# Where the result's scatters are issued in a two-layer graph network on one core

## The chip, the cores and the metric

The kernel runs on one core of a Trainium2 chip. A core has five engines that run side by side, each through its own list of instructions in order: PE (TensorE, matrix products), DVE (VectorE), ACT (ScalarE), POOL (GpSimd) and SP (SyncE, here only issuing transfers). Data move between memory and the on-chip buffers by DMA transfers, which are issued from SP, ACT or POOL. A transfer whose rows are picked by a list of indices (an indirect one: a gather reads such rows, a scatter writes them) is issued from POOL here.

The metric is the device time of one execution, in microseconds (us). It was 4598.26 us, the median of three runs (4597.88 to 4599.86).

## What is computed

A graph of 6250 nodes with 128 features each and 206,250 edges. A first layer spreads the features five times along the edges, then projects and normalises. A second layer is an attention over the edges of each node. Cut to what matters:

```python
def _L1_gnn_ref(node_attr, edge_attr, edge_sh, ..., edge_index):
    src, dst = (edge_index[0], edge_index[1])
    q = (node_attr @ Wq).reshape(n, H, DQ // H)
    x_src = node_attr[src]
    k = _conv_per_edge(x_src, edge_attr, edge_sh, Wang_k, Wlin_k, W1k, b1k, W2k)
    v = _conv_per_edge(x_src, edge_attr, edge_sh, Wang_v, Wlin_v, W1v, b1v, W2v)
    alpha = jnp.einsum('ehq,qk,ehk->eh', q[dst], Wdot, k)
    ...                      # softmax of alpha over the edges of each dst
    out = jax.ops.segment_sum(attn[..., None] * v, dst, num_segments=n)
    return out.reshape(n, DV) @ Wout

x = _layernorm(x + _L0_gnn_ref(x, edge_index, L0_gnn_weight, L0_gnn_bias), axis=-1)
x = _layernorm(x + _L1_gnn_ref(x, edge_attr_16, edge_attr_16_n2, ..., edge_index), axis=-1)
return x
```

The change lies in the second layer, at the end of it: how the rows of the final `x` get to memory.

## The kernel before

The first half of the run sorts and counts edges and runs the first layer (`count_rows`, `propagate`). While the first layer runs, `order_nodes` ranks the nodes by their number of edges and `lay_edges` lays the edge data out in that order. In `lay_edges`, the text of the program issues for each tile one gather of source indices (L639, into `src_all`) and one or more gathers of edge rows (L643, into `ea_l`, a tile with six buffers), then writes them back transposed (L668).

The second half is `attend`. Nodes stand in the order of their rank, 128 to a tile, 49 tiles (0 to 48). Tile `t` has `WIDTHS[t]` slots: slot `j` holds the `j`-th edge of each of its 128 nodes. The widths fall from 64 to 22 and sum to 1658. Slots are worked on in groups of up to four that don't cross a tile's end: 433 groups. One loop of iterations `i` runs over the groups, and in each iteration stands, in this order:

- `fetch(i + 3)`: on SP the edge data; on POOL one gather per slot (L788), which brings the 128 source nodes' rows from `x1_d` into `xs`. `xs` has six buffers, one group each. A buffer comes free when its group's transposes are done.
- `nets(i)`, `radial(i - 1)`, `turn(i + 1)`, `keys(i - 1)`: the per-edge products on PE, DVE and ACT. `turn` holds the transposes of the gathered rows (L817), which are the last use of an `xs` buffer.
- `step(running)`, two or three times: carries `softmax(t)` of the tile before one `yield` further. So the softmax of a tile is spread over about nine iterations of the next tile's groups.

At its end `softmax(t)` writes the tile's rows to `z[:, t, :]` (L922, DVE) and their statistics. `z` holds all 49 tiles and is used once. After tiles 12, 25, 38, 45, 47 and 48 (`NORMS`, L47) it normalises all tiles since the last time: L933 on DVE, one instruction per tile, and right behind each L933 the scatter of that tile's 128 rows to `out`, by the node numbers in `rows` (L937, POOL). Batches are thus 13, 13, 13, 7, 2 and 1 scatters. Inside a batch there is a `yield` after every fourth tile (`u % 4 == 3`). The scatters are declared free of one another, since every node has one place.

The order of PE, DVE and ACT is that of the text: L53 names them in `MANUAL`, and the loop runs inside `tc.manual_schedule(engines=MANUAL)`. POOL and SP aren't named there; the order of their lists is made by the compiler, which takes account of what depends on what and of which buffers are free.

Of the kernel before, what the change touches and what calls it, by code (L numbers as in the profile page):

```python
# [18 lines left out]
P = 128  # L19
N = 6250  # L20
# [123 lines left out]
def stats(nc, work, z, v):  # L144
    st = work.tile([P, nc.vector.BN_STATS_DIM], F32, name="st")
    nc.vector.bn_stats(st, z)
    nc.vector.bn_aggr(v, st)
# [567 lines left out]
def attend(tc, w1, b1, wang, w2, wlin, wqd, wout, ident, rows, c_iota, src_all, eas_o, x1_d, x1_r, out):  # L715


    nc = tc.nc
    WM = WIDTHS[0]
    with ExitStack() as s:  # L720
        one = s.enter_context(tc.tile_pool(name="at1", bufs=1))
# [30 lines left out]
        nc.vector.tensor_scalar(none, degf, 0.0, None, OP.is_equal)  # L752
        z = one.tile([P, NT, D], F32, name="z")
        v = one.tile([P, NT, 2], F32, name="v2")
        puts = []
        kvs = [one.tile([P, WIDTHS[i], DK + D], F32, name=f"kv{i}") for i in range(2)]

        groups = [(t, j, min(4, w - j)) for t, w in enumerate(WIDTHS) for j in range(0, w, 4)]
# [3 lines left out]
        def ps(name):  # L762
            return pp.tile([P, CH], F32, name=name, tag="ps")
# [6 lines left out]
        def fetch(g):  # L770
            t, j, n = groups[g]
            if j == 0:
                x1s[t] = three.tile([P, D], F32, name="x1s")
                nc.sync.dma_start(x1s[t], x1_r[t * P:(t + 1) * P, :])
            if j % SC == 0:

                c, s, m = pieces(t)[j // SC]
                ea[t, c] = three.tile([P, 4, SC * 32], FR, name="ea")
                for i in range(8):
                    at = (i % 4 // 2) * 32 + i // 4 * 16  # L780
                    nc.sync.dma_start(
                        ea[t, c][16 * i:16 * i + 16, :, :m * 32].bitcast(F32),
                        bass.AP(tensor=eas_o.tensor, offset=eas_o.offset + (at * OFFS[NT] + s) * P,
                                ap=[[OFFS[NT] * P, 16], [m * 32, 4], [1, m * 32]]))
            xs[g] = deep.tile([P, 4, D], F32, name="xs")
            for i in range(n):
                c = OFFS[t] + j + i
                nc.gpsimd.indirect_dma_start(  # L788
                    out=xs[g][:, i, :], out_offset=None, in_=x1_d[:, :],
                    in_offset=bass.IndirectOffsetOnAxis(ap=src_all[:, c:c + 1], axis=0))  # L790
# [52 lines left out]
        def radial(g):  # L843

            t, j, n = groups[g]
            r = r1.pop(g)
            p_r = pp.tile([P, 2, CH], F32, name="p_r")
            for i in range(n):
                u = i % 2 * (DK + D)
                nc.tensor.matmul(p_r[:, i // 2, u:u + DK + D], r[:, i, :], w2_s, start=True, stop=True)  # L850
            rr[g] = two.tile([P, 4, DK + D], F32, name="rr")
            r2 = rr[g].rearrange("p (b i) f -> p b (i f)", i=2)
            for b, f in banks(n):
                nc.scalar.copy(r2[:, b, :f], p_r[:, b, :f])  # L854

        def keys(g):
# [12 lines left out]
            for b, f in banks(n):  # L869
# [5 lines left out]
            nc.vector.tensor_reduce(al[t][:, j:j + n], a[:, :, :DK].rearrange("p j (h k) -> p j h k", h=H),  # L875
                                    AX.X, OP.add)

        def softmax(t):

            w = WIDTHS[t]  # L880
            a = kv[t]
            l = al.pop(t)[:, :w]
            ex = two.tile([P, WM, H], F32, name="ex")
            m = two.tile([P, H], F32, name="m")
            d = two.tile([P, H], F32, name="d")
            nc.vector.tensor_tensor(l, l, keep[t][:, :w, None].to_broadcast([P, w, H]), OP.min)
            nc.vector.tensor_reduce(m, l.rearrange("p j h -> p h j"), AX.X, OP.max)
            nc.vector.tensor_tensor(l, l, m[:, None, :].to_broadcast([P, w, H]), OP.subtract)
            yield
            nc.scalar.activation(ex[:, :w], l, AF.Exp)  # L890
            yield
            nc.vector.tensor_tensor(ex[:, :w], ex[:, :w],
                                    ok[t][:, :w, None].to_broadcast([P, w, H]), OP.mult)
            nc.vector.tensor_reduce(d, ex[:, :w].rearrange("p j h -> p h j"), AX.X, OP.add)
            nc.vector.tensor_scalar(d, d, none[:, t:t + 1], None, OP.add)
            nc.vector.reciprocal(d, d)
            yield

            for u in range(0, w, 8):
                k = min(8, w - u)  # L900
                av = a[:, u:u + k, DK:].rearrange("p j (h f) -> p j h f", h=H)
                nc.vector.tensor_tensor(av, av, ex[:, u:u + k, :, None].to_broadcast([P, k, H, D // H]),  # L902
                                        OP.mult)
                yield
                if u > 0:
                    nc.vector.tensor_add(a[:, :k, DK:], a[:, :k, DK:], a[:, u:u + k, DK:])
                    yield
            for h in (4, 2, 1):
                nc.vector.tensor_add(a[:, :h, DK:], a[:, :h, DK:], a[:, h:2 * h, DK:])  # L909
            yield  # L910
            av = a[:, :1, DK:].rearrange("p j (h f) -> p j h f", h=H)
            o = two.tile([P, H, D // H], F32, name="o")
            nc.vector.tensor_tensor(o, av[:, 0], d[:, :, None].to_broadcast([P, H, D // H]), OP.mult)
            yield
            tr = ps("tr4")
            nc.tensor.transpose(tr[:, :P], o.rearrange("p h d -> p (h d)"), ident)
            oT = two.tile([P, P], F32, name="oT")
            nc.scalar.copy(oT, tr[:, :P])
            yield
            y = ps("y4")  # L920
            nc.tensor.matmul(y[:, :D], oT, wo, start=True, stop=True)
            nc.vector.tensor_add(z[:, t, :], x1s.pop(t), y[:, :D])  # L922
            stats(nc, two, z[:, t, :], v[:, t, :])
            if t + 1 in NORMS:
                yield
                t0 = NORMS[NORMS.index(t + 1) - 1]
                rs = two.tile([P, NT], F32, name="rs")
                n = t + 1 - t0
                nc.vector.tensor_scalar(rs[:, :n], v[:, t0:t + 1, 1], EPS, None, OP.add)
                nc.scalar.activation(rs[:, :n], rs[:, :n], AF.Sqrt)  # L930
                nc.vector.reciprocal(rs[:, :n], rs[:, :n])
                for u in range(t0, t + 1):
                    nc.vector.tensor_scalar(z[:, u, :], z[:, u, :], v[:, u, 0:1],  # L933
                                            rs[:, u - t0:u - t0 + 1], OP.subtract, OP.mult)

                    k = min(P, N - u * P)
                    st = nc.gpsimd.indirect_dma_start(  # L937
                        out=out[:, :], in_=z[:k, u, :], in_offset=None,
                        out_offset=bass.IndirectOffsetOnAxis(ap=rows[:k, u, 0:1], axis=0)).ins
                    for q in puts:  # L940
                        tc.declare_no_dep(st, q, reason="a node has one place in the order")
                    puts.append(st)
                    if u % 4 == 3:
                        yield

# [2 lines left out]
        def step(of):  # L948
            if of and next(of[0], None) is None and of[0].gi_frame is None:
                of.pop(0)  # L950

        with tc.manual_schedule(engines=MANUAL):
            for i in range(-3, len(groups) + 1):
                live = [0 <= i + x < len(groups) for x in range(-1, 4)]
                if live[4]:
                    fetch(i + 3)
                if live[1]:
                    nets(i)
                step(running)
                if live[0]:  # L960
                    radial(i - 1)
                if live[2]:
                    turn(i + 1)
                step(running)
                if live[0]:
                    keys(i - 1)
                    t, j, n = groups[i - 1]
                    if j + n == WIDTHS[t]:
                        running.append(softmax(t))
                if len(running) > 1:  # L970
                    step(running)
                if live[3] and groups[i + 2][1] == 0:
                    begun.append(begin(groups[i + 2][0]))
                step(begun)
            for r in running:
                for _ in r:
                    pass


def attend_any(tc, w1, b1, wang, w2, wlin, wqd, wout, c_heads, c_sum, ident, last, srct, dstt, eat,  # L980
# [368 lines left out]
```

## Time and profile before

| | us |
|---|---|
| median of three runs | 4598.26 |
| the profiled execution, in all | 4606.73 |
| its span, first to last instruction | 4604.9 |
| attention stage: first gather L788 starts | 2315.69 |
| last gather L788 starts / ends | 4557.74 / 4558.69 |
| last scatter L937 starts | 4592.12 |
| batches of scatters start | 3116.60, 3729.38, 4268.58, 4534.52, 4578.19, 4592.12 |

The busy time of the engines by stage, in us:

| stage (us from the span's start) | PE | DVE | ACT | POOL | granted PE clock |
|---|---|---|---|---|---|
| 0 to 430 (sorting, counting) | 187 | 346 | 111 | 92 | 0.88 |
| 430 to 1005 (edge counts) | 403 | 494 | 334 | 56 | 0.78 |
| 1005 to 2315 (first layer) | 1243 | 948 | 701 | 478 | 0.98 |
| 2315 to 4605 (attention) | 1951 | 1963 | 906 | 1728 | 0.95 |

A row of the list of groups reads: line, engine, operation, what it writes and reads, how many; after the bar the busy time and the mean duration of one in ns; after the next bar the engine's idle time just before these instructions, and what ended it. "issue" is time in which the engine waited for nothing that the profile shows. A row of a timeline reads: start, duration, engine, line, operation, and in brackets the gap before it and what ended the gap. In a row for a stretch the columns after its length are busy time and number of instructions, the granted PE clock, the busy share of the transfer engines and GB/s.

### The profile page before, as it was taken

To read this page: it belongs to the slowest core of one execution; us is meant where nothing else is said; L and a number is where in the kernel's file an instruction comes from. 1 tells how busy PE (TensorE), PEld (TensorE's weight loads), DVE (VectorE), ACT (ScalarE), POOL (GpSimd) and SP (SyncE) were. 2 spreads that over 40 slices of the span, in tenths; PEclk is the share of its full clock that TensorE was granted. 3 is DMA by queue.
4 is the path that set the end of the run, shared out by engine and by line. 5 is a ranking of instruction groups with operands and counts; after the bars stand their busy time and mean duration, and the time that the engine had idled before them with its cause. 6 is when DMAs were issued, how large, how long until landed. Compare 5 with 4: busy or idle time off the path is not lost.

```text
span 4604.9 us, 73118 instructions
## 1 busy us (share of the span) xinstructions
PE 3785.5 (82%) x24823; PEld 3371.9 (73%) x24823; DVE 3751.0 (81%) x5996; ACT 2051.8 (45%) x4137; POOL 2353.1 (51%) x2343
## 2 busy tenths in 40 slices
PE   4345554997999999999868898987888878888886
PEld 4345554886888888787667788887888868787785
DVE  8769996865787787766649898987988988899887
ACT  0046664644656566464334343443443433444333
POOL 0340000056333344303277777777777777777774
PEclk9986766998999999999989999999999999999898
DMA  8023334555877788765365455554555555555442
GB/s 296 9 50 78 80 78 115 150 155 164 238 229 229 222 233 247 230 174 155 111 125 101 98 102 101 103 99 97 102 100 100 106 97 105 102 103 102 90 100 48
DMA packets 389736, 601.64 MB, mean 131 GB/s; under 512 B 120093, under 2 KB 325205, under 8 KB 378554
## 3 DMA queue, kind: packets, MB, share of 16 engines
q1 hardware_dynamic: 256570, 356.98, 32.0%
q0 software_dynamic: 127056, 204.67, 19.4%
q10 hardware_dynamic: 5728, 35.22, 2.3%
q8 instruction: 201, 3.29, 0.3%
q14 instruction: 181, 1.48, 0.1%
HBM read 491.89 MB, written 132.25 MB: 136 GB/s over the span
## 4 chain that ended last, share of the span: by engine, by line
PE 23%; DVE 11%; DMA 8%; POOL 7%; issue 5%; ACT 1%; SPq 0%; DVEq 0%; POOLq 0%; ACTq 0%
DMA xs<-x_d,src_all 7%; PE p_r L850 6%; POOL xs L788 6%; PE p_k L866 5%; PE p_k L864 3%; DVE mkv L839 3%; DVE kv L871 3%; PE acc L444 3%; PE p_g L831 2%; PE p_x L817 1%; DVE kv L902 1%; DVE kv L909 1%; DVE kv L873 1%; PE p_h L831 1%; POOL x_r L368 1%
## 5 line engine op out<-in xcount | busy, mean ns | idle before, releaser
L788 POOL DMA_INDIRECT xs<-x_d,src_all x1658 | 1676.7, 1011 | 505.5 <-issue 423.1
L444 PE MATMUL acc<-c,parts 128*128 128x512 f32 (+1 forms) x6370 | 1411.1, 382 | 78.9 <-DVE c L427 42.8
L444 PEld LDWEIGHTS acc<-c,parts 128*128 128x128 f32 x6370 | 1154.3, 189 | 305.8 <-DVE c L427 48.9
L427 DVE CAST c<-c 128x1024 fp32r<-128x1024 uint8 x980 | 683.8, 716 | 240.1 <-PE acc L444 196.2
L866 PE MATMUL p_k<-wlin_s,mkv 128*128 128x128 f32 x3316 | 755.4, 310 | 0.0
L440 ACT CAST c<-c 128x512 fp32r<-128x512 uint8 x735 | 456.2, 623 | 561.5 <-PE acc L444 441.9
L864 PE MATMUL p_k<-wlin_s,mkv 128*128 128x64 f32 x3316 | 581.1, 258 | 65.7 <-DVE kv L871 64.8
L850 PE MATMUL p_r<-w_s,r 128*128 128x192 f32 x3316 | 619.9, 330 | 0.0
L850 PEld LDWEIGHTS p_r<-w_s,r 128*128 128x128 f32 x3316 | 571.2, 194 | 34.4 <-issue 0.2
L864 PEld LDWEIGHTS p_k<-wlin_s,mkv 128*128 128x128 f32 x3316 | 523.1, 199 | 95.0 <-DVE kv L871 94.1
L871 DVE TENSOR_TENSOR kv<-rr,p_k 128x768 f32<-128x768 f32 (+2 forms) x443 | 397.1, 898 | 205.6 <-PE p_k L866 189.0
L854 ACT COPY rr<-p_r 128x768 f32<-128x768 f32 (+2 forms) x443 | 335.3, 759 | 476.8 <-PE p_r L850 462.2
L839 DVE TENSOR_TENSOR mkv<-p_g,xT 128x512 f32<-128x512 f32 (+3 forms) x866 | 534.2, 659 | 7.0 <-PE p_g L831 6.9
L866 PEld LDWEIGHTS p_k<-wlin_s,mkv 128*128 128x128 f32 x3316 | 523.5, 199 | 0.0
L228 PE MATMUL p_c<-oh_h,oh_l 128*128 128x100 bf16 x3136 | 301.1, 273 | 263.3 <-DVE oh_h L153 199.5
L833 ACT ACTIVATE r<-p_h,b_s 128x512 f32<-128x512 f32 (+3 forms) x433 | 290.6, 671 | 464.1 <-PE p_h L831 456.4
L228 PEld LDWEIGHTS <-oh_l 128*128 128x128 bf16 x3136 | 289.3, 124 | 272.2 <-DVE oh_h L153 208.0
L668 POOL DMA_DIRECT2D eas_o<-eT_l x252 | 204.9, 816 | 505.2 <-DVE eT_l L662 490.7
L817 PE MATMUL p_x<-ident,xs 128*128 128x128 f32 x1658 | 276.9, 279 | 131.7 <-DMA xs<-x_d,src_all 123.2
L230 ACT CAST cT<-p_c 128x500 uint8<-128x500 f32 (+1 forms) x637 | 306.8, 644 | 118.1 <-DVE c_row L236 61.1
L817 PEld LDWEIGHTS p_x<-ident,xs 128*128 128x128 f32 x1658 | 212.2, 142 | 164.4 <-DMA xs<-x_d,src_all 122.6
L820 ACT COPY xT<-p_x 128x512 f32<-128x512 f32 (+3 forms) x433 | 248.6, 574 | 135.9 <-PE p_x L817 131.9
(195 smaller groups left out, 4524.8 us busy)
## 6 DMA issues: line engine op xcount, KB each, us to landing
c<-counts SPq DMA_DIRECT2D x360, 384.0 KB
ea<-eas_o SPq DMA_DIRECT2D x648, 128.0 KB
c<-counts SPq DMA_DIRECT2D x120, 448.0 KB
eas_o<-eT_l POOLq DMA_DIRECT2D x162, 256.0 KB
counts<-c_row SPq DMA_DIRECT2D x588, 48.0 KB
xs<-x_d,src_all POOLq DMA_INDIRECT x1658
eat<-in_eas ACTq DMA_DIRECT2D x1, 25792.0 KB
counts<-c_row SPq DMA_DIRECT2D x196, 56.0 KB
```

Source lines behind the costliest of these rows:

```text
L228: nc.tensor.matmul(p_c[:, q - q0], oh_los[t % 2][:, q // Q, :, q % Q], oh_hi[:, q // Q, :, q % Q], start=True, stop=True)
L427: nc.vector.tensor_copy(c[:, u:u + 1024].rearrange("p (n b x) -> p n b x", n=2, b=2), r[:, :, v:v + 512].rearrange("p b (n x) -> p n b x", ...
L440: nc.scalar.copy(c[:, 1024:w].rearrange("p (b x) -> p b x", b=2), r[:, :, 512:])
L444: nc.tensor.matmul(a[:, :v - u], parts[:, j, i, :], c[:, u:v], start=(j == 0 and i == 0), stop=(j == NT - 1 and i == 1))
L788: nc.gpsimd.indirect_dma_start(out=xs[g][:, i, :], out_offset=None, in_=x1_d[:, :], in_offset=bass.IndirectOffsetOnAxis(ap=src_all[:, c:c ...
L817: nc.tensor.transpose(p_x[:, i * P:(i + 1) * P], xs[g][:, i, :], ident)
L839: nc.vector.tensor_tensor(mkv[g][:, i, :n].rearrange("p j (b e) -> p b j e", b=4), p_g[:, i, :n * P].rearrange("p (b j e) -> p b j e", b=4 ...
L850: nc.tensor.matmul(p_r[:, i // 2, u:u + DK + D], r[:, i, :], w2_s, start=True, stop=True)
L854: nc.scalar.copy(r2[:, b, :f], p_r[:, b, :f])
L864: nc.tensor.matmul(p_k[:, i // 2, u:u + DK], m[:, 0, i, :], wlin_s[:, :DK], start=True, stop=True)
L866: nc.tensor.matmul(p_k[:, i // 2, u + DK:u + DK + D], m[:, 1, i, :], wlin_s[:, DK:], start=True, stop=True)
L871: nc.vector.tensor_mul(k.rearrange("p (b i) f -> p b (i f)", b=b.stop - b.start), r2[:, b, :f], p_k[:, b, :f])
```

## The change

`softmax` no longer issues a tile's scatter behind its L933. It notes the tile in a list `done`. A new function `store` issues the scatters of the noted tiles and empties the list. The loop calls it at the end of an iteration only from `i + 3 >= len(groups)` on, that is once no `fetch` follows in the text, and then behind each further step of the softmaxes that are still running. The instruction itself is the same, and so are its operands and the declaration that scatters are free of one another.

```diff
-        puts = []
+        puts, done = [], []
...
+        def store():
+
+            for u in done:
+
+                k = min(P, N - u * P)
+                st = nc.gpsimd.indirect_dma_start(
+                    out=out[:, :], in_=z[:k, u, :], in_offset=None,
+                    out_offset=bass.IndirectOffsetOnAxis(ap=rows[:k, u, 0:1], axis=0)).ins
+                for q in puts:
+                    tc.declare_no_dep(st, q, reason="a node has one place in the order")
+                puts.append(st)
+            done.clear()
...
                 for u in range(t0, t + 1):
                     nc.vector.tensor_scalar(z[:, u, :], z[:, u, :], v[:, u, 0:1],
                                             rs[:, u - t0:u - t0 + 1], OP.subtract, OP.mult)
-
-                    k = min(P, N - u * P)
-                    st = nc.gpsimd.indirect_dma_start(
-                        out=out[:, :], in_=z[:k, u, :], in_offset=None,
-                        out_offset=bass.IndirectOffsetOnAxis(ap=rows[:k, u, 0:1], axis=0)).ins
-                    for q in puts:
-                        tc.declare_no_dep(st, q, reason="a node has one place in the order")
-                    puts.append(st)
+                    done.append(u)
                     if u % 4 == 3:
                         yield
...
                 step(begun)
+                if i + 3 >= len(groups):
+                    store()
             for r in running:
                 for _ in r:
-                    pass
+                    store()
+                store()
```

## The prediction

> **What bounds the kernel now.** I read the list of groups for POOL alone over the attention stage first, then the table of waits of that stage, then POOL's timeline at the places where the scatters stand.
>
> ```profile
> 2315.60:4558.70 2243.10, 1723.77 (x1704) 0.96 0.53 101
> L788 POOL DMA_INDIRECT xs<-x_d,src_all x1658 | 1676.7, 1011 | 505.5 <-issue 423.1 <-DMA xs<-x_d,src_all 38.9 <-PE p_x L817 21.9
> L937 POOL DMA_INDIRECT out<-z,rows x49 | 50.7, 1035 | 45.3 <-DVE z L933 31.0 <-issue 7.0 <-DMA out<-z,rows 2.7
> POOL xs L788 <- issue: 423.1, 1388, 0.4
> ```
>
> The first line is POOL's busy time from the first gather to the end of the last: 1723.77 us in 1704 instructions (1658 gathers and 46 scatters) of 2243.10. The remaining 519.3 us are 1704 gaps of 0.305 us. The last line gives the longest such gap as 0.4 us: POOL never stands still for a buffer, an engine or a transfer. A gather costs 2181.0/1657 = 1.316 us from start to start, and POOL's chain of 1704 issues sets when the last gather leaves. Other engines have room: in the same stretch PE is busy 1937 us and DVE 1935 us of 2243 (86%), and PE's transposes at L817 wait 123.2 us for gathered rows in the run. After the last gather 46.2 us remain.
>
> ```profile
> 3095.69 2.15 DVE L933 TENSOR_SCALAR z<-z,v,rs 128x128 f32<-128x128 f32 x8
> ...
> 3115.08 1.21 POOL L788 DMA_INDIRECT xs<-x_d,src_all  x1 [0.30 <-issue]
> 3116.60 1.01 POOL L937 DMA_INDIRECT out<-z,rows  x1 [0.31 <-issue]
> ...
> 3125.84 1.20 POOL L937 DMA_INDIRECT out<-z,rows  x1 [0.30 <-DMA out<-z,rows]
> 3127.34 0.99 POOL L788 DMA_INDIRECT xs<-x_d,src_all  x1 [0.30 <-PE p_r L850]
> 3128.64 0.99 POOL L788 DMA_INDIRECT xs<-x_d,src_all  x1 [0.30 <-issue]
> 3129.94 1.00 POOL L937 DMA_INDIRECT out<-z,rows  x1 [0.30 <-issue]
> ```
>
> Start, duration, engine, line; the bracket is the gap before. Eight scatters, two gathers, five scatters. Counting POOL's rows from 2315.69, 611 gathers lie before the first scatter. The program text has it elsewhere: tile 12's normalisation falls in iteration 151, by which `fetch` has issued groups 0 to 154, that is the 583 slots of tiles 0 to 13 and 12 more, 595. The 16 extra gathers are groups 155 to 158. Group 158 takes the buffer of group 152, whose transposes (`turn(i+1)`) stand in iteration 151: POOL's list had run as far ahead as the six `xs` buffers allow. The next two batches stand after 1063 and 1461 gathers, in the text after 1047 and 1445: again 16 more. The fourth begins after 1646 (text 1632), in the middle of the last group the buffers allow.
>
> So the compiler orders POOL (it isn't among the `MANUAL` engines of L53) by what is ready, not by place in the text. A second place shows how far it goes:
>
> ```profile
> 1035.37 1.02 POOL L643 DMA_INDIRECT ea_l<-eat,at_l  x1 [0.30 <-issue]
> 1036.70 1.02 POOL L639 DMA_INDIRECT src_all<-srct,at_l  x1 [0.30 <-issue]
> 1038.02 1.19 POOL L639 DMA_INDIRECT src_all<-srct,at_l  x1 [0.30 <-issue]
> ...
> L639 POOL DMA_INDIRECT src_all<-srct,at_l x49: 950/955/1829, 1025.2 to 1102.9; - x49
> L643 POOL DMA_INDIRECT ea_l<-eat,at_l x126: 957/1080/1705, 1027.4 to 1946.0; - x126
> ```
>
> In the text each L639 stands just ahead of its tile's first L643. In the trace six L643 go out (their tile has six buffers), then L639 of later tiles run one after another: all 49 by 1102.9, while the L643 go on to 1946.0. When the loop has no free buffer, work that needs none is drawn forward from far behind it.
>
> **The change part by part.** The 49 scatters are the same instructions with the same operands. In the text 46 of them move behind all 1658 gathers; the last three (tiles 46 to 48) already stand there. Nothing is added on PE, DVE, ACT or SP: their lists hold the same instructions in the same order.
>
> (a) *The move.* A scatter needs its row block of `z` (L933) and nothing that is scarce: no `xs` buffer. The eight L933 from 3095.69 run in 2.15 us without waiting for any scatter between them in the text, although they write the same tile: the dependence goes by region. So scatter 0 is ready in the compiler's order where it was, and POOL's list was out of gathers there. I expect the first 39 in the same stretches, at most spread over several groups because a freed buffer's gathers now go first. They stay ahead of the last gather: 0 us.
>
> (b) *The last batch.* Tiles 39 to 45 have ten gathers left behind them:
>
> ```profile
> 4534.52 1.00 POOL L937 DMA_INDIRECT out<-z,rows  x1 [0.30 <-issue]
> 4535.82 0.98 POOL L788 DMA_INDIRECT xs<-x_d,src_all  x1 [0.30 <-issue]
> ...
> 4544.78 0.97 POOL L937 DMA_INDIRECT out<-z,rows  x1 [0.30 <-issue]
> 4546.05 0.99 POOL L788 DMA_INDIRECT xs<-x_d,src_all  x1 [0.30 <-PE p_k L866]
> ...
> 4557.74 0.95 POOL L788 DMA_INDIRECT xs<-x_d,src_all  x1 [0.30 <-issue]
> 4578.19 1.10 POOL L937 DMA_INDIRECT out<-z,rows  x1 [19.50 <-DVE z L933]
> 4579.60 1.00 POOL L937 DMA_INDIRECT out<-z,rows  x1 [0.31 <-DVE al L888]
> 4592.12 1.57 POOL L937 DMA_INDIRECT out<-z,rows  x1 [11.53 <-DVE z L933]
> ```
>
> Each of the seven that slips behind the last gather lets that gather out one scatter earlier. The 46 scatters take 61.0 us start to start, 1.327 each. From none to all seven: 0 to -9.3 us. Behind the last gather they cost nothing as long as the 19.50 us gap (waiting for DVE's z of tile 46) covers them, and 9.3 fits; without that gap they would cost the 9.3 back. Six of them stood in one stretch between groups 429 and 430, so the nearest row says that nearly all stay; I take one: -1.3.
>
> (c) *Changes of kind on POOL.* The first instructions after a change between gathers and scatters are longer: 1.01 and 1.02 against 0.97 for scatters (the first batch), 0.99 and 0.99 against 0.95 for gathers, together 0.17 us a visit. There are six visits now before the last gather, at most 46 if every scatter stood alone: 0 to 40 x 0.17 = +6.8. Six and thirteen scatters stood together before without a gather between them, so I take 0.
>
> (d) *Waits.* POOL runs in order, so a scatter that waits holds up the gathers queued behind it, and PE's L817 behind those. Now scatter 0 starts 20 us after its z began (3095.69 to 3116.60) and is not waited for. At unchanged places that stays: 0. If the compiler put them about 16 gathers sooner, the margin would be gone; but they can't be ready sooner than now.
>
> Sum: 4604.9 + 0 - 1.3 + 0 + 0 = 4603.6 us of span. The profiled execution took 4606.73 in all, 8.5 above the median of 4598.26; taking the difference over to the median, 4598.26 - 1.3 = 4597.0.
>
> One rule of the Trainium skill bears on what a moved issue is worth. DMA: Bandwidth & Descriptors, section "Anatomy of one DMA", puts most of a small DMA's fixed 2 us in the completion, with about 50 ns for the sequencer and little for building descriptors; as an estimate from that, 46 issues would hold POOL for 46 x 0.05 = 2.3 us and no order of them could matter. The rows here say 0.97 us busy and 0.30 between, 61.0 us for the 46; the measurement decides.
>
> **The rivals.**
>
> *The order follows the text (faster).* Then the last gather leaves 61.0 us sooner, 46 scatters follow it back to back from 4558.99 - 61.0 = 4498.0 to 4559.0, then tiles 46, 47 and 48, whose z is ready by 4592.1 - 61.0 = 4531.1, at 1.33 each. The last would start at 4561.7, where it now starts at 4592.12; with the same 12.8 us after it the span is 4574.4, -30.5: 4567.8 of median. For it: the text, and a POOL that never idles. Against it: the two places above where POOL's order departs from the text as soon as buffers run out.
>
> *The order follows the text and the gathers were not what held the stage (slower).* Then PE or DVE takes over as bound, and the last gather doesn't leave sooner; it waits for a buffer instead. All 49 scatters would follow it, the last at 4558.99 + 48 x 1.327 = 4622.7 in place of 4592.12: +30.6, 4628.9. It turns from gain to loss where the last gather gains less than 30.6 of the 61.0 us. For it: PE and DVE at 86%, and a granted clock that falls at times. Against it: 61 us is 2.7% of the stage, less than the 14% that they have free, and the transposes wait on gathers now.
>
> **How the numbers follow.** My forecast, that the compiler draws the scatters forward and little changes, has a chance of 0.84; the text's order with its gain 0.10; with its loss 0.06. The time is the forecast's, 4597. Its ends are -9.3 and +6.8 on 4598.26, 4589.0 and 4605.1; with 1 us for the spread of the three runs, 4588 to 4606. That leaves out the two rivals, 0.16, and little more, so it is the range. About 0.2% (9.2 us) is what a measurement of this kernel can tell from no change. Faster by more: 0.10 from the rival and 0.01 from the forecast's lower end; slower by more: 0.06; the same: 0.83.
>
> **What would show it.** In the changed kernel's POOL timeline: the first scatter after about 611 gathers, near 3116, and batches near 3729 and 4268; the last gather near 4557; after it at most seven scatters and then a gap of 10 to 19 us before tile 46's. If a run of 46 scatters follows the last gather, step (a) is wrong, and the time then tells which rival. If scatters stand alone between groups and the rows near them are longer, (c) was undersized. If POOL shows a gap of several us before a scatter with DVE z as the releaser, (d) was.

## The result and the profile after

Over 12 executions of each kernel, side by side, the kernel before took 4599.12 us and the changed one 4601.09 (medians): ratio 1.0003, 95% interval 0.9994 to 1.0013. That is no change that can be measured. The forecast was 4597.0, in a range of 4588 to 4606.

The profiled execution of the changed kernel has a span of 4603.1 us (4604.9 before). The scatter has become L883, its L933 has become L946. First the row of the stage, from the first gather to the end of the last; its columns are length, then busy time and instructions of PE, its weight loads, DVE, ACT and POOL, then the clock, the share of the transfer engines and GB/s:

```profile
2315.20:4556.80 2241.60, 1943.54 (x13114) 1780.47 (x13115) 1935.37 (x3429) 896.44 (x1509) 1722.17 (x1704) 0.96 0.52 101
```

The groups of POOL in the same stretch, and its waits there (total, how many, longest):

```profile
L788 POOL DMA_INDIRECT xs<-x_d,src_all x1658 | 1675.1, 1010 | 505.7 <-issue 426.1 <-DMA xs<-x_d,src_all 37.2 <-PE p_x L817 19.5
L883 POOL DMA_INDIRECT out<-z,rows x46 | 47.1, 1024 | 14.0 <-issue 6.1 <-DMA xs<-x_d,src_all 1.8 <-DVE kv L871 1.5
```

```profile
POOL xs L788 <- issue: 426.1, 1397, 0.3
```

1704 instructions lie in the stretch, as before: 1658 gathers and still 46 scatters. No scatter has left the stage. POOL is still without a pause (519.4 us of gaps, 0.305 each, the longest 0.3), and the stretch is 1.5 us shorter than before (2241.60 against 2243.10).

POOL's timeline shows where the scatters went. The first batch, and the end of the run:

```profile
3113.30 1.22 POOL L788 DMA_INDIRECT xs<-x_d,src_all  x1 [0.30 <-issue]
3114.82 1.00 POOL L883 DMA_INDIRECT out<-z,rows  x1 [0.30 <-issue]
...
3124.06 1.20 POOL L883 DMA_INDIRECT out<-z,rows  x1 [0.30 <-DMA out<-z,rows]
3125.57 0.98 POOL L788 DMA_INDIRECT xs<-x_d,src_all  x1 [0.31 <-PE p_r L850]
...
3129.41 0.95 POOL L788 DMA_INDIRECT xs<-x_d,src_all  x1 [0.30 <-issue]
3130.67 1.00 POOL L883 DMA_INDIRECT out<-z,rows  x1 [0.30 <-issue]
3131.98 0.99 POOL L883 DMA_INDIRECT out<-z,rows  x1 [0.30 <-DMA xs<-x_d,src_all]
...
4548.12 1.00 POOL L883 DMA_INDIRECT out<-z,rows  x1 [0.30 <-issue]
4549.43 1.09 POOL L788 DMA_INDIRECT xs<-x_d,src_all  x1 [0.30 <-DMA xs<-x_d,src_all]
...
4555.85 0.95 POOL L788 DMA_INDIRECT xs<-x_d,src_all  x1 [0.31 <-issue]
4576.32 1.09 POOL L883 DMA_INDIRECT out<-z,rows  x1 [19.52 <-DVE z L946]
4577.71 0.98 POOL L883 DMA_INDIRECT out<-z,rows  x1 [0.30 <-DVE al L901]
4590.23 1.57 POOL L883 DMA_INDIRECT out<-z,rows  x1 [11.54 <-DVE z L946]
```

Counted through, the scatters stand behind these numbers of gathers:

| | first batch | second | third | fourth | last three |
|---|---|---|---|---|---|
| before | 611: 8, 613: 5 | 1063: 13 | 1461: 13 | 1646: 1, 1648: 6 | 1658 |
| after | 611: 8, 615: 2, 619: 3 | 1063: 4, 1067: 6, 1071: 3 | 1461: 7, 1465: 6 | 1648: 6, 1652: 1 | 1658 |

The change of the text has split the batches into portions between groups of four gathers, and nothing else. Ten portions stand ahead of the last gather, where six stood before; behind it are the same three scatters.

### The profile page after: what moved, and what is told of

It reads as the page before. It is cut to its first block, busy times and chain, and to the rows that moved or that the text cites. A ratio compares the mean times of both kernels' runs of the same rounds, so it can differ in the third digit from the quotient of the medians.

```text
span 4603.1 us, 73118 instructions
## 1 busy us (share of the span) xinstructions
PE 3795.4 (82%) x24823; PEld 3382.2 (73%) x24823; DVE 3749.5 (81%) x5996; ACT 2047.5 (44%) x4137; POOL 2352.0 (51%) x2343
## 4 chain that ended last, share of the span: by engine, by line
PE 21%; DMA 9%; DVE 9%; POOL 8%; issue 6%; ACT 1%; POOLq 0%; DVEq 0%; ACTq 0%
DMA xs<-x_d,src_all 9%; POOL xs L788 7%; PE p_r L850 5%; PE p_k L866 5%; PE p_k L864 3%; PE acc L444 3%; DVE mkv L839 2%; DVE kv L871 2%; PE p_g L831 2%; PE p_x L817 1%; PE p_h L831 1%; DVE kv L922 1%; DVE kv L915 1%; DVE kv L873 1%; POOL x_r L368 1%
## 5 line engine op out<-in xcount | busy, mean ns | idle before, releaser
L864 PE MATMUL p_k<-wlin_s,mkv 128*128 128x64 f32 x3316 | 580.9, 258 | 56.6 <-DVE kv L871 55.4
L850 PE MATMUL p_r<-w_s,r 128*128 128x192 f32 x3316 | 623.1, 331 | 0.0
L850 PEld LDWEIGHTS p_r<-w_s,r 128*128 128x128 f32 x3316 | 575.2, 195 | 35.4 <-issue 0.4
L871 DVE TENSOR_TENSOR kv<-rr,p_k 128x768 f32<-128x768 f32 (+2 forms) x443 | 396.7, 897 | 205.5 <-PE p_k L866 189.3
```

What stands on the lines that cost most here:

```text
L864: nc.tensor.matmul(p_k[:, i // 2, u:u + DK], m[:, 0, i, :], wlin_s[:, :DK], start=True, stop=True)
L871: nc.vector.tensor_mul(k.rearrange("p (b i) f -> p b (i f)", b=b.stop - b.start), r2[:, b, :f], p_k[:, b, :f])
```

## The experiments

The mechanism to be tested has two halves. One: the compiler puts a scatter where POOL has run out of gathers that have a free buffer, whatever the text says. The other is the price: what it would have been worth if the scatters had really gone behind the gathers (the faster rival's -30.5 us). Twelve runs were made in four groups, each group on one chip together with the kernel before. On these chips the kernel before took 5091.44, 5098.53, 5136.94 and 5095.58 us, not 4599. So each kernel is compared with the kernel before of its own group, and what differs there is taken up first.

**The kernel before, on such a chip.**

> The kernel before, for its profile on this chip. If this chip hands work over between engines later than the one of the first profile, the gathers' stage takes some 2600 us from first to last gather (2242 in the first profile) with POOL waiting some 200 us for PE's transposes; if POOL is without gaps also here, the 490 us more lie in the stages ahead of 2315.

One execution, 5143.69 us. The stage's row and POOL's waits in it:

```profile
2369.00:5069.90 2700.90, 2095.84 (x12980) 1902.66 (x12981) 1923.96 (x3385) 874.21 (x1492) 1723.54 (x1704) 0.89 0.42 84
```

```profile
POOL xs L788 <- issue: 431.7, 1391, 4.5
POOL xs L788 <- PE p_x L817: 279.0, 111, 6.7
POOL xs L788 <- remote: 131.2, 64, 6.0
```

What lies ahead of the first gather is 53 us longer (2369.00 against 2315.69), the gathers' stage 458 us (2700.90 against 2243.10), what follows the last gather 26 us (72.0 against 46.2). POOL's busy time is the same (1723.54 against 1723.77), and DVE's within 1%; POOL now waits 279.0 us for the transposes that free `xs`, and 131.2 us for something that the profile shows only as "remote". POOL is no longer without gaps here. The counts of gathers ahead of the scatters are those of the first profile. The whole kernel after had the same counts too, and no other time than before:

> The kernel after, unchanged, beside the kernel before on this chip. The theory that the compiler keeps the place of the scatters: 0.999 to 1.001 of the kernel before, portions at 611, 1063, 1461 and 1648 gathers. If the places mattered only where the queue of the gathers has gaps: up to 0.5% off.

Measured: 5134.95 us, ratio 0.9994 (0.9973 to 1.0015), portions behind 611, 615, 619, 1063, 1067, 1071, 1461, 1465, 1648 and 1652 gathers. So the case's result holds on this chip also.

**Does the number of buffers set the place?** The changed kernel with two more `xs` buffers:

```diff
-        deep = s.enter_context(tc.tile_pool(name="at_x", bufs=6))
+        deep = s.enter_context(tc.tile_pool(name="at_x", bufs=8))
```

> The changed kernel with eight xs buffers in place of six. Theory (the compiler draws scatters forward where its gathers run out of buffers): the first scatters stand after 611 + 8 = 619 gathers, the next after 1071 and 1469, in similar portions; the time is as before within 0.2%, since POOL issues as many instructions ahead of the last gather. Rival (their place is set by when z is ready and has nothing to do with the buffers): first scatters still after about 611.

Measured: 5092.47 us, ratio 1.0009 (0.9989 to 1.0028). The batches begin behind 619, 1071, 1469 and 1656 gathers: each exactly eight later, two groups of four. If the readiness of `z` alone set the place, it would have stayed at 611. In the order that the compiler makes, a scatter comes up once the gathers with a free buffer are used up. One of the fourth batch's seven now stands behind the last gather.

**The scatters really behind the gathers.** Each scatter is bound behind the last gather in POOL's list:

```diff
+                gathers.append(nc.gpsimd.indirect_dma_start(
...
-                st = nc.gpsimd.indirect_dma_start(
+                with (tc.issue_after(gathers[-1]) if u >= 0 else ExitStack()):
+                    st = nc.gpsimd.indirect_dma_start(
```

> The changed kernel, with each scatter bound in POOL's issue order behind the last gather, so that the order which the change's text has is also the order that POOL gets. Theory (POOL's chain of issues sets the attention stage, and the change did nothing because the compiler drew the scatters forward): 1658 gathers stand in one run, then 49 scatters; the last gather leaves 61 us sooner, near 4497, the 31 us that POOL idles behind it (19.5 and 11.5) are filled with scatters, span about 4574, 30 us or 0.66% faster than before. Rival (the gathers are not what held the stage; PE or DVE bound): the last gather stays near 4557, the scatters come behind it, up to 31 us slower. Second rival (scatters cost POOL nothing that matters): no change.

> The same kernel as e1_all_behind once more. There the kernel before took 5091 us in place of 4599, POOL waited 244 us for PE's transposes to give buffers free, and engines waited up to 27 us for one another while scatters went out. If this run shows POOL without gaps in the attention stage again (the kernel before near 4599), the theory of the POOL chain asks for -30 us, 0.66% faster. If hand-offs between engines are held up by a burst of scatters also there, the burst of 46 behind the last gather holds up the last groups and the gain is lost: 0 to 30 us slower than that. If the kernel before is near 5090 again, no change, as in e1_all_behind.

> The kernel after with all 49 scatters bound behind the last gather, a third time, for a chip where the kernel before takes 4600 us as in the first profile, if the run falls on such a one. There POOL issues without a gap, and a portion of scatters holds no hand-over between the other engines up: the faster rival's sum says 4568, ratio 0.993. If the tail gives back there too what the stage gains, the ratio is 1.000 as in the two runs before, and this is expected (0.997 to 1.001) on a chip where the kernel before takes over 5050 us.

Measured, on three chips: ratios 0.9992 (0.9972 to 1.0012), 0.9987 (0.9971 to 1.0003) and 0.998 (0.9958 to 1.0002). In each trace all 49 scatters stand behind 1658 gathers. The move that the text describes is done; each interval holds 1 and shuts out the 30 us (ratio 0.994). Where the gain went is seen beside the next kernel, which leaves the rows of tiles 0 to 45 unwritten:

```diff
             for u in done:
+                if u < 46:
+                    continue
```

> The changed kernel without the scatters of tiles 0 to 45; those rows of the result are not written. It measures what 46 scatters cost where they stand. Theory: 46 issues of 1.33 us leave POOL's chain, the last gather goes out 61 us sooner and the 46 us behind it stay as they are: span about 4542, 1.3% faster than before. Rival (stage not bound by POOL): less than half of that.

> The same kernel as e3_left_out once more (without the scatters of tiles 0 to 45). With POOL's chain as the bound: 61 us less, 1.3%. With POOL waiting for buffers and the kernel before near 5090: 1.1% less, as in e3_left_out.

Measured: ratios 0.9888 (0.9863 to 0.9914) and 0.988 (0.986 to 0.990), or 58 and 65 us less for 46 scatters. The last gather of POOL's timeline, first with the scatters behind, then without them on the same chip:

```profile
4955.92 0.95 POOL L788 DMA_INDIRECT xs<-x_d,src_all  x1 [0.30 <-issue]
```

```profile
4964.29 1.02 POOL L788 DMA_INDIRECT xs<-x_d,src_all  x1 [0.30 <-issue]
```

So the stage of the gathers gains about all that taking the scatters out of it can give (the 8 us between the two are less than executions of one kernel differ by there, 5072.67 to 5122.95 for the kernel before). But the span goes on for 129.0 us after the last gather with them behind it, and 64.6 us without them. The second chip shows the same: last gathers at 4971.59 and 4959.68, and 122.0 and 68.5 us behind them. The row of the stretch with the 46 scatters, and that of the rest (all behind, first of its three runs):

```profile
4957.20:5016.30 59.10, 14.77 (x62) 12.78 (x63) 9.01 (x17) 4.04 (x7) 45.37 (x46) 0.61 0.16 51
5016.30:5085.90 69.60, 27.48 (x163) 23.84 (x161) 41.26 (x83) 15.58 (x26) 3.61 (x3) 0.67 0.02 5
```

For 59.1 us POOL issues scatters, and DVE does 17 instructions; the 69.60 us that follow are a whole tail again (64.60 us without the scatters). Rows picked from the timeline of the same stretch show the other engines' waits:

```profile
4958.06 0.69 ACT L833 ACTIVATE r<-p_h,b_s 128x512 f32<-128x512 f32 x1 [0.51 <-PE p_x L817]
...
4959.60 0.44 PE L866 MATMUL p_k<-wlin_s,mkv 128*128 128x128 f32 x2
...
4963.72 0.80 ACT L854 COPY rr<-p_r 128x768 f32<-128x768 f32 x1 [4.98 <-remote]
...
4967.75 2.76 PE L850 MATMUL p_r<-w_s,r 128*128 128x192 f32 x8
...
4980.03 0.95 DVE L871 TENSOR_TENSOR kv<-rr,p_k 128x768 f32<-128x768 f32 x1 [16.86 <-remote]
...
5013.56 0.80 ACT L854 COPY rr<-p_r 128x768 f32<-128x768 f32 x1 [26.55 <-remote]
...
5015.30 0.97 POOL L884 DMA_INDIRECT out<-z,rows  x1 [0.30 <-issue]
5059.36 1.07 POOL L884 DMA_INDIRECT out<-z,rows  x1 [43.09 <-DVE z L947]
```

DVE's L871 at 4980.03 needs `rr` (written by 4964.52) and `p_k` (done by 4960.04): it starts 15.5 us after both. ACT's copy at 5013.56 takes a `p_r` that ended at 4970.51, and L871 had read both `rr` buffers by 4980.98; ACT had stood idle for 26.55 us. The instructions of DVE and ACT last as long as elsewhere (0.95, 0.80). PE's eight L850 take 2.76 us in place of 1.46 at 4954.34, at a granted clock of 0.61 in this stretch; these 1.3 us don't make up the 15 to 26. What is late is the hand-over between engines, as long as POOL issues without a pause. The Trainium skill, SBUF — State Buffer, section "SBUF: two separate sides", names one way in which POOL can block others: it and DVE share a pair of ports, which POOL's and some of DVE's instructions lock for their whole length, while PE and ACT have their own. That doesn't fit here: ACT is held too, by 26.55 us, DVE's own instructions aren't longer, and no scatter of the stretch lasts more than 1.69 us.

**Part of them behind.** Only the scatters of tiles 35 to 48 are bound behind the last gather (`if u >= 35`), eleven more than the three that always stood there:

> The changed kernel, with only the scatters of tiles 35 to 45 (eleven) bound behind the last gather; the others stay where the compiler puts them. Theory (what is won is POOL idle time behind the last gather that gets filled): eleven issues of 1.33 us, 14.6 us, fit into the 19.5 us of idle, so the last gather leaves 14.6 us sooner and the end with it: 0.32% faster than before. Rival (it is the batches of 13 in the middle of the stage that hurt, by starving PE): no gain here, or only a part of it.

> The same kernel as e5_eleven_behind once more (eleven scatters bound behind the last gather). With POOL's chain as the bound: 14.6 us less, 0.32%. With POOL waiting for buffers and the kernel before near 5090: no change.

Measured: 0.9997 (0.998 to 1.0015) and 0.9982 (0.9966 to 0.9998). The 14.6 us of the theory would be a ratio of 0.9971; the first interval shuts that out, the second doesn't. On the chip of the two traces above the last gather starts at 5006.45, 50.5 us later than with all behind, and what remains after it is 76.4 us against 129.0. The 35 scatters that stay ahead cost the stage about what they save the tail.

**One at a time.** If it were long portions that hold the others up, single scatters should be cheaper. The first 39 are each bound to a gather of their own:

```diff
+                at = (620 + 34 * u if u < 13 else 1070 + 30 * (u - 13) if u < 26 else 1465 + 14 * (u - 26))
+                with (tc.issue_after(gathers[at]) if u < 39 else ExitStack()):
```

> The kernel after, but each of the first 39 scatters is bound to a gather of its own: about one scatter after every 34, 30 and 14 gathers of the three stretches, instead of portions of 6 to 8; the last ten as they are. If a scatter costs its own time of the queue wherever it stands (46 left out brought 57 to 65 us), the median is that of the kernel before within 0.3%. If it is the portions that hold up the other engines (in the run of 49 behind the gathers the others waited 26 and 47 us for events that were past), singles cost less: 0.4 to 0.8% below the kernel before.

Measured: 0.9995 (0.9978 to 1.0011), with 39 scatters alone between gathers in the trace. So on these chips a scatter costs about its own time of POOL's queue, alone or in a portion, ahead of the last gather or behind it: 58 and 65 us for 46 of them are 1.3 to 1.4 us each, the time from one to the next.

**The order of the text.** Both rivals supposed that POOL follows the text. The kernel before, with all of POOL's gathers and scatters bound to each other in the order of its text:

```diff
+                with (tc.issue_after(issued[-1]) if issued else ExitStack()):
+                    ld = nc.gpsimd.indirect_dma_start(
...
+                issued.append(ld)
...
+                    with tc.issue_after(issued[-1]):
+                        st = nc.gpsimd.indirect_dma_start(
...
+                    issued.append(st)
```

> The kernel before with POOL's gathers and scatters bound in the order of its text (8 scatters after 595 gathers, 5 more by 599, 13 by 1051, 13 by 1445, 10 by 1630, 3 at the end). The theory that a scatter costs its own time wherever it stands: the kernel before within 0.3%. If the order of the text is what hurts (a scatter ahead of its z holds the gathers behind it): 1 to 3% slower, with POOL's idle time ahead of the scatters put down to DVE's z.

Measured: 5193.51 us, ratio 1.0104 (1.0085 to 1.0124), 56.6 us more than the kernel before. The first scatter of each batch in POOL's timeline:

```profile
3327.35 1.08 POOL L940 DMA_INDIRECT out<-z,rows  x1 [16.93 <-issue]
...
4082.13 1.11 POOL L940 DMA_INDIRECT out<-z,rows  x1 [15.90 <-DVE z L935]
...
4745.63 0.99 POOL L940 DMA_INDIRECT out<-z,rows  x1 [20.43 <-DVE z L935]
...
5080.35 1.00 POOL L940 DMA_INDIRECT out<-z,rows  x1 [17.14 <-DVE z L935]
```

POOL stands four times, 70.4 us together, for a `z` that isn't there yet, with the gathers queued behind the scatter. The first is put down to "issue", but L935 writes its `z` from 3326.19 on, 1.2 us before it starts. In the kernel before the same scatters start without a wait. Bound like this, the batches begin behind 595, 1047, 1441 and 1628 gathers; in the kernel before behind 611, 1063, 1461 and 1646. The 16 to 20 gathers by which the compiler runs ahead (16 x 1.3 = 21 us) are what covers this wait. The 56.6 us aren't that wait alone: behind the first batch DVE and ACT stand 18.56 and 24.63 us for something "remote" while POOL issues gathers, so the price may be another on a chip like that of the first profile.

## Why the prediction held

**Step (a), the move: shown.** The batches stand behind 611, 1063, 1461 and 1648 gathers, starting at 3114.82, 3729.66, 4270.17 and 4535.35, where the prediction named 611 and times near 3116, 3729 and 4268. The spread over several groups is there too. The run with eight buffers shows its reason, that the place is set by free buffers. One count of the prediction is off: in the text the third and fourth batch begin behind 1441 and 1628 gathers, as the run in the order of the text shows, not 1445 and 1632; only the rest of each batch stands there. So the compiler is 16 to 20 gathers ahead, not 16 throughout. Nothing in the sum rests on it.

**Step (b), the last batch: -1.3 taken, 0 found.** None of the seven slipped behind the last gather; the end of its range with no slip was right. The last gather starts at 4555.85 in place of 4557.74; these 1.9 us are less than executions of one kernel differ by (before: 4594.97 to 4609.86). For the same reason the 1 us that the range allowed for spread was too little for single executions (after: 4595.26 to 4612.38); the median lies inside.

**Step (c), changes of kind: right within what shows.** There are ten visits before the last gather in place of six, four more; at 0.17 each 0.7 us. The gathers went out every 1.315 us from start to start, 1.316 before.

**Step (d), waits: 0, shown, and its warning too.** No scatter waits longer than 0.31 us until the gathers are out. The prediction held that the margin of some 20 us would be gone if the scatters stood 16 gathers sooner; the text's order does just that and waits 15.9 to 20.4 us at each of four places.

**The rivals.** Neither happened, as the order doesn't follow the text. Their prices were tried where the order was forced. The faster rival's -30.5 didn't come: the stage of the gathers gave about what it said (50.5 us between 35 scatters ahead and none), but the sum had the last tiles' `z` ready 61 us sooner while the scatters run, and on those chips little runs beside them. The slower rival's reason, gathers that gain less than half, didn't come either. The three ratios have a mean of 0.9986, about 7 us; each interval holds 1.

**What stays open.** Whether -30.5 us could be had on a chip like that of the first profile. There, the other engines go on while a portion is issued, and stand behind it. The second batch of 13 scatters in the kernel before and the 17.2 us that follow, with the same columns, of the first profile and then of the profile on an experiments' chip:

```profile
3729.40:3746.60 17.20, 9.09 (x62) 7.90 (x60) 14.63 (x26) 4.92 (x8) 13.24 (x14) 0.95 0.17 51
3746.60:3763.80 17.20, 11.29 (x58) 9.85 (x59) 3.51 (x7) 3.05 (x6) 13.24 (x14) 0.65 0.20 53
```

```profile
4079.20:4096.40 17.20, 11.57 (x57) 10.28 (x55) 8.70 (x21) 3.78 (x5) 13.20 (x14) 0.71 0.17 51
4096.40:4113.60 17.20, 10.09 (x51) 9.61 (x52) 7.14 (x11) 4.04 (x6) 10.88 (x12) 0.70 0.57 97
```

DVE is busy 14.63 of 17.20 us during the batch in the first and 8.70 in the other. Behind it the first falls to 3.51, for want of the rows that the batch put off, as two rows of the first profile show:

```profile
3749.42 0.45 PE L817 MATMUL p_x<-ident,xs 128*128 128x128 f32 x1 [9.73 <-DMA xs<-x_d,src_all]
...
3756.96 0.95 DVE L871 TENSOR_TENSOR kv<-rr,p_k 128x768 f32<-128x768 f32 x1 [12.55 <-PE p_k L866]
```

So a batch holds up the stage there too, but by the gathers behind it and not by late hand-overs; behind the last gather there would be none. No run with the scatters behind fell on a chip of the first kind, so what they would cost there isn't shown. Why the hand-overs are late on the others is open as well.

## What to carry to other kernels

Where the compiler makes an engine's order, moving an instruction in the text need not move it: look in the trace for what it ran out of (here buffers) when it drew the instruction forward, and if another place is wanted, bind it and look again. A text that puts an in-order queue's work behind a fresh result costs the wait for that result, once for each batch; a lead of other work ahead of it covers that. And before an issue is moved "behind" the bound queue, ask what is left to run there: what the stage gains, the tail can give back.

## What the runs showed of the hardware that was not expected

The same kernel takes 4599 us in the first measurement and 5091 to 5137 on the four chips of the experiments. POOL's and DVE's busy times agree; PE's is longer in the gathers' stage (2095.84 us against 1937.46), at a granted clock of 0.89 against 0.96; and the waits called "remote" are there on the four chips only (131.2 us for POOL alone in that profile, none in the first two). While POOL issues indirect transfers one behind the other, an engine there can stand 15 to 26 us after all that it needs is done. It doesn't take scatters: in the run without 46 of them ACT's longest "remote" wait is 20.30 us, up to 2410.06, and POOL issues gathers without a pause from 2365.41 to 2405.38; from 2450 to the last gather no such wait of ACT, DVE or POOL is longer than 9.4 us.
